# Turning the input in slices 3, 4 and 7 of a chunk instead of 0, 2 and 4

## The chip, the cores and the metric

The kernel runs on one core of one Trainium2 chip. Its time is the device time in microseconds (us). The core has five engines that run side by side, each through its own list of instructions in order: TensorE (PE in the profile; PEld is its loading of weights), VectorE (DVE), ScalarE (ACT), GpSimd (POOL) and SyncE (SP), which here only issues DMAs.

## The reference

The input x is 16 images of 56 x 56 pixels with 384 channels, in float32. Two layers follow each other, each with a residual:

```python
x = x + attention(groupnorm(x), w_qkv, w_proj, b_proj)   # layer 0
x = x + depthwise3x3(groupnorm(x), sign(w))              # layer 1
```

`groupnorm` takes mean and variance of 32 groups of 12 channels over a whole image. The attention projects each pixel to q, k and v (1152 x 384 weights), and lets each pixel look at 3 x 3 neighbours: 12 heads of 32 channels, in three groups with dilations 1, 2 and 3. The softmax runs over the nine neighbours of each head; the weighted sum of v is projected (384 x 384) and added to x. Layer 1 is a 3 x 3 convolution per channel, whose weights are the signs of the given ones.

## The kernel before

**Tiling.** An image is cut into 7 chunks of 8 rows (448 pixels), so there are 112 chunks, `m = 7 b + c` with image b and chunk c. On chip a chunk lies as channels x pixels, in three blocks of 128 channels. Every matmul on 448 pixels in float32 is two PE instructions.

**Stages.** `plan_a` (L402) is stage A: load a chunk of x (pixels on partitions), turn it (`turn`, L420: four PE transposes per channel block into a PSUM tile `pt_x`, a ScalarE copy `xa`, L435, and VectorE's statistics, L436), and write it to DRAM as `xd` (L438). `plan_b` (L446) is stage B: load `xd`, normalise it, project k, v (`pkv`) and q (`pq`, all L464), multiply q by the nine shifted k (L517), sum over channels on PE (the scores, `ps`, L502), softmax (`softmax_1` to `softmax_5`, L529 to L563: the score copy `sT`, PE transposes `pt_s`, L535, maximum, exponential, sum, L544, division, L546, and a split into three bfloat16 terms, on ScalarE and GpSimd), a transposing DMA (`aT`, L568), spreading of the weights to channels on PE (`pb_a`, L581, in nine bursts of three matmuls a chunk), VectorE's product of each burst with v (`w`, L588), GpSimd's adds (L596, L599, L600), the output projection (`po`, L614) and the residual with the statistics of layer 1 (L617, L620). `plan_c` (L648) is stage C: load the result `x1d`, normalise it (L698, L741), convolve (two channel blocks on PE, `pc`, L712; the third on ScalarE and GpSimd, L770 to L786), turn it back (`pt_o`, L793) and store it.

**Order.** Nothing is issued by loop order. `at(when, order, piece)` (L392) puts each piece of work into a table; at the end all pieces are issued by `when`, and within one `when` by `order`, from SOFTMAX (0) to LOADS (14); STAGE_A is 11, behind the projections and ahead of STAGE_C. A chunk has STEP = 9 values of `when`, here called slices 0 to 8. Stage B of chunk m begins at `9 m`, stage C at `9 (m + 10)`, stage A at `start_a(m)`, from the third image on `9 (m - 12)` or one more; so in one round of nine slices PE scores chunk m, turns chunk m + 12 and convolves chunk m - 10. A scheduler then places the issued instructions on each engine's list by its own estimate of times, with the issue order as priority; a list's order is fixed when the program is built.

**Buffers.** The input tile `xin` has one buffer (a second tile is borrowed for the chunks in `doubled`, L852). The three PSUM buffers of `ps_mt` go round among `pt_x`, `pkv`, `po`, `pt_s`, `pc`, `pt_o` and the small tiles of the statistics. `pb_a`, `pq` and `ps` have one PSUM buffer each: a burst of `pb_a` waits until VectorE has multiplied the burst before.

**Statistics.** `statistics` (L858) plans a group norm's finish: aggregating the chunks' statistics (`channels`, L306), then mean, deviation, variance, inversion and spreading, at the distances STAT_SLICE. For the first two images it is planned from the slice of their last turn (L879); for later ones from stage B (L883), together with layer 1's of two images before. It falls into the rounds of c = 0 and c = 1.

Of the kernel before, what the change touches and what calls it, by code (L numbers as in the profile page):

```python
# [20 lines left out]
NG = 3  # L21
# [14 lines left out]
def dilated_attention_then_binary_conv(  # L36
# [31 lines left out]
    NCH = H // ROWS  # L68
# [151 lines left out]
    def turn_qkv_weights(cc):  # L220
        for t3 in range(3):
            pt = ps_mt.tile([P, 512], F32, tag="mt", name="pt_wq")
            for i in range(3):
                nc.tensor.transpose(pt[:, i * P : (i + 1) * P], raw["q", t3][:, i, cc * P : (cc + 1) * P], ident)
            nc.scalar.copy(wqkvT[:, cc, t3 * C : (t3 + 1) * C], pt[:, :C])

    def turn_proj_weights(cc):
        pt = ps_mt.tile([P, 512], F32, tag="mt", name="pt_wp")
        for i in range(3):
            nc.tensor.transpose(pt[:, i * P : (i + 1) * P], raw["p"][:, i, cc * P : (cc + 1) * P], ident)  # L230
        nc.vector.tensor_copy(wprojT[:, cc, :], pt[:, :C])
# [155 lines left out]
    def chunk_of(dram, c):  # L387
        return dram.rearrange("(j p) n -> p j n", p=P)[:, :, c * PX : (c + 1) * PX]
# [3 lines left out]
    def at(when, order, piece):  # L392

        pieces.setdefault((when, order), []).append(piece)
# [7 lines left out]
    def plan_a(m, t0):  # L402

        b, c = divmod(m, NCH)
        had = {}

        def load():
            if c == 0:
                stats0[b] = st_p.tile([P, NG, NCH, 6], F32, tag="stats0", name="stats0")
                xd[b] = dr_p.tile([C, H * W], F32, tag="xd", name="xd")  # L410
            if (b == 0 and c % 3) or m in doubled:

                xin = z_p.tile([P, NQ * PX], F32, tag="z", name="xin_z")[:SUB, : NSUB * C]
                xin = xin.rearrange("p (s c) -> p s c", s=NSUB)
            else:
                xin = xin_p.tile([SUB, NSUB, C], F32, tag="xin", name="xin")
            had["xin"] = xin
            nc.sync.dma_start(xin, xf[b, c * PX : (c + 1) * PX, :].rearrange("(s p) c -> p s c", p=SUB))

        def turn(j):  # L420
            pt = ps_mt.tile([P, 512], F32, tag="mt", name="pt_x")
            for s in range(NSUB):
                nc.tensor.transpose(  # L423
                    pt[:, s * SUB : (s + 1) * SUB], had["xin"][:, s, j * P : (j + 1) * P], ident[:SUB, :SUB]
                )
            if b == 0:

                if j == 0:
                    pool, tag = ((xn_p, "xn"), (xn_p, "xn"), (xn_p, "xn"), (xr_p, "xr"), (t_p, "t"), (w_p, "w"),
                                 (w_p, "w"))[c]  # L430
                    first[c] = pool.tile([P, NG, PX], F32, tag=tag, name="x_first")
                xa = first[c][:, j]
            else:
                xa = xa_p.tile([P, PX], F32, tag="xa", name="xa")
            nc.scalar.copy(xa, pt[:, :PX])  # L435
            nc.vector.bn_stats(stats0[b][:, j, c, :], xa)  # L436
            if b:
                nc.sync.dma_start(xd[b][j * P : (j + 1) * P, c * PX : (c + 1) * PX], xa)  # L438
            elif j == NG - 1:
                nc.scalar.dma_start(chunk_of(xd[b], c), first[c])  # L440

        at(t0 - 3 if b else FIRST + 2 * max(c - 2, 0), LOADS, load)
        for j in range(NG):
            at(t0 + 2 * j if b else FIRST + 2 * c + 1, STAGE_A, lambda j=j: turn(j))

    def plan_b(m, t0):  # L446

# [389 lines left out]
    STAT_ORDER = (STATISTICS, SPREAD, SPREAD, SPREAD, STATISTICS, SPREAD)  # L837
    STEP = 9
    STAT_SLICE = (0, 1, 2, 4, 5, 7)
    FIRST = -200  # L840
    at(FIRST, LOADS, load_weights)
    for cc in range(NG):
        at(FIRST + 6 + 2 * cc, STAGE_C, lambda cc=cc: turn_qkv_weights(cc))
        at(-21 + cc, STAGE_C, lambda cc=cc: turn_proj_weights(cc))
# [9 lines left out]
    def start_a(m):  # L854
        behind = max(m - AHEAD, -2 + m - NCH - len([d for d in doubled if d <= m]))
        return STEP * (behind if m >= NCH else m - 9) + (m in doubled)

    def statistics(when, sets):  # L858

        steps = {}  # L860

        def norm(k, *which):
            if not steps:
                steps["of"] = group_norm([
                    (stats1[b], lambda mr, mrz, b=b: mr1.update({b: (mr, mrz)}), True) if layer
                    else (stats0[b], lambda mr, b=b: mr0.update({b: mr}), False)
                    for layer, b in sets
                ])
            steps["of"][k](*which)

        for n, (layer, _) in enumerate(sets):
            for j in range(NG):

                sooner = 3 - j if n and not layer else 0
                at(when - sooner, STATISTICS, lambda n=n, j=j: norm(0, n, j))
        for k in range(1, 6):
            at(when + STAT_SLICE[k], STAT_ORDER[k], lambda k=k: norm(k))

    for b in range(2):  # L879
        statistics(start_a(NCH * b + NCH - 1) + 5, [(0, b)])  # L880
    for b in range(B):
        last = NCH * b + NCH - 1
        statistics(STEP * last + 27, [(1, b)] + ([(0, b + 2)] if b + 2 < B else []))  # L883
    for m in range(N):
        plan_a(m, start_a(m))
        plan_b(m, STEP * m)
        plan_c(m, STEP * (m + 10))
# [31 lines left out]
```

## Time and profile before

The time is 5223.8 us, the median of three runs (5223.65 to 5231.6). The profiled execution took 5223.35 us.

| | before |
|---|---|
| profiled execution, us | 5223.35 |
| its span, first to last instruction, us | 5221.6 |
| mean granted clock of TensorE | 0.984 |
| busy us of PE, PEld | 5085.7, 2322.5 |
| busy us of DVE, ACT, POOL | 4199.0, 2310.7, 4242.2 |
| turns: PE transposes L423 (1344 in all), us from start to start | 0.095 |
| copies of turns, ACT L435, `xa` x315, mean ns | 534 |
| statistics of turns, DVE L436, median ns | 618 |
| loads of x, L418, 672 KB each, us to landing | 7.3 |

The profile shows one execution. A row of the timeline has the start in us from the span's start, the duration, the engine, the line, the operation with output and inputs, and how many such instructions are merged; a bracket gives the time the engine stood idle before it and what ended that. In the table of waits the columns are total us, times and the longest. PE's instructions overlap, so the distance of two starts tells more than a duration. The forty digits are tenths of busy time in forty equal slices of the span.

### The profile page before, as it was taken

The page shows a single profiled execution, that of the slowest core. Times are in us where ns is not written, and L with a number is a line of the kernel's source. Part 1 is how long each engine was busy: PE and PEld are TensorE (multiplying, and loading weights), DVE is VectorE, ACT ScalarE, POOL GpSimd, SP SyncE. Part 2 cuts the span into 40 slices and gives each one's busy share as a digit, 9 for nine tenths or more (in the row PEclk, how much of TensorE's full clock was granted, in tenths as well). Part 3 has the DMA queues.
Part 4 walks back from the last instruction along what each step waited for, and adds up shares of the span by engine and source line. Part 5 has one row for each costly group of instructions (what it writes and reads, how often), then busy time and mean ns, then how long its engine had stood idle before and what let it go on. Part 6 is the DMA issues. An engine that isn't in the chain of part 4 may idle for free. (4 is left out here: it accounts for less than half of the span.)

```text
span 5221.6 us, 75614 instructions
## 1 busy us (share of the span) xinstructions
PE 5085.7 (97%) x26885; PEld 2322.5 (44%) x26885; DVE 4199.0 (80%) x4125; ACT 2310.7 (44%) x4077; POOL 4242.2 (81%) x2950
## 2 busy tenths in 40 slices
PE   8999999999999999999999999999999999999976
PEld 4444444444444444444444444444444444444433
DVE  4898888888888888888888888888888888878764
ACT  3223444444444544444444444444445444444444
POOL 2677878888888888889888888888888888888881
PEclk8999999999999999999999999999999999999987
DMA  6444656666566565656666565665666656554445
GB/s 197 127 124 119 167 160 166 163 166 167 162 169 165 161 163 159 168 158 166 166 166 165 163 166 162 165 163 160 164 163 171 167 163 168 141 138 135 121 135 158
DMA packets 811631, 825.62 MB, mean 158 GB/s; under 512 B 360307, under 2 KB 801014, under 8 KB 811254
## 3 DMA queue, kind: packets, MB, share of 16 engines
q1 hardware_dynamic: 803270, 808.79, 56.9%
q10 hardware_dynamic: 7984, 12.00, 0.7%
q8 instruction: 213, 3.49, 0.3%
q14 instruction: 164, 1.34, 0.1%
HBM read 466.41 MB, written 231.21 MB: 134 GB/s over the span
## 5 line engine op out<-in xcount | busy, mean ns | idle before, releaser
L596 POOL TENSOR_TENSOR w<-w 128x1344 f32<-128x1344 f32 x672 | 2048.7, 3049 | 327.3 <-DVE w L588 279.1
L517 DVE TENSOR_TENSOR t<-pq,k 128x1344 f32<-128x1344 f32 x1008 | 1528.6, 1550 | 237.8 <-PE pq L464 236.6
L588 DVE TENSOR_TENSOR w<-pb_a,v 128x1344 f32<-128x1344 f32 x1008 | 1560.3, 1548 | 172.6 <-PE pb_a L581 91.9
L464 PE MATMUL pkv<-xn,wqkvT 128*128 128x448 f32 x3924 | 1542.2, 542 | 3.9 <-ACT xa L435 3.5
L464 PEld LDWEIGHTS pkv<-xn,wqkvT 128*128 128x128 f32 x3924 | 725.9, 190 | 664.7 <-issue 634.7
L614 PE MATMUL po<-y,wprojT 128*128 128x448 f32 x2016 | 834.9, 550 | 17.3 <-POOL y L600 17.3
L464 PE MATMUL pq<-xn,wqkvT 128*128 128x448 f32 x1962 | 834.9, 560 | 0.0
L698 ACT ACTIVATE z<-z,mrz 96x448 f32<-96x448 f32 x840 | 573.9, 751 | 266.0 <-DMA z<-x1d 239.7
L777 POOL TENSOR_TENSOR m<-m 128x1344 f32<-128x1344 f32 x210 | 639.1, 3044 | 43.3 <-ACT m L770 37.9
L502 PE MATMUL ps<-t,sel 128*32 128x448 f32 x6048 | 660.8, 546 | 0.3 <-DVE t L517 0.2
L474 ACT COPY v<-pkv 128x448 f32<-128x448 f32 x336 | 178.1, 530 | 918.3 <-PE pkv L464 911.1
L770 ACT ACTIVATE m<-zg,ktap 128x448 f32<-128x448 f32 x945 | 552.6, 658 | 15.1 <-POOL m L777 5.7
L614 PEld LDWEIGHTS po<-y,wprojT 128*128 128x128 f32 x2016 | 376.1, 191 | 374.1 <-issue 347.1
L712 PE MATMUL pc<-z,kdiag 96*32 96x440 f32 (+1 forms) x5040 | 519.3, 545 | 7.1 <-POOL z L700 4.3
L464 PEld LDWEIGHTS pq<-xn,wqkvT 128*128 128x128 f32 x1962 | 345.2, 190 | 318.8 <-issue 318.8
L617 DVE SCALAR_TENSOR_TENSOR xr<-po,bias,xr 128x448 f32<-128x448 f32 x336 | 227.9, 678 | 277.8 <-PE po L614 272.7
L435 ACT COPY xa<-pt_x 128x448 f32<-128x448 f32 x315 | 167.4, 534 | 618.2 <-PE pt_x L423 618.2
L558 POOL TENSOR_TENSOR rest<-ew,e 112x512 f32<-112x512 f32 x112 | 130.1, 1162 | 358.9 <-ACT e L554 358.9
L581 PE MATMUL pb_a<-aT,spread 24*128 24x448 bf16 x3024 | 369.5, 360 | 42.7 <-DVE w L588 36.7
L600 POOL TENSOR_TENSOR y<-y,w 128x448 f32<-128x448 f32 x336 | 381.7, 1136 | 23.8
L599 POOL TENSOR_TENSOR y<-w 128x448 f32<-128x448 f32 x336 | 382.8, 1139 | 19.3
L581 PEld LDWEIGHTS <-spread 24*128 24x128 bf16 x3024 | 100.8, 91 | 621.4 <-issue 603.6
(132 smaller groups left out, 4307.6 us busy)
## 6 DMA issues: line engine op xcount, KB each, us to landing
z<-x1d SPq DMA_DIRECT2D x570, 224.0 KB, 4.0
xr<-xd SPq DMA_DIRECT2D x112, 672.0 KB, 4.3
x1d<-xr SPq DMA_DIRECT2D x112, 672.0 KB, 3.2
xn<-xd SPq DMA_DIRECT2D x109, 672.0 KB, 4.5
xin<-in_x_dram SPq DMA_DIRECT2D x105, 672.0 KB, 7.3
xd<-xa SPq DMA_DIRECT2D x315, 224.0 KB, 3.2
out_dram<-osb SPq DMA_DIRECT2D x420, 168.0 KB, 3.4
x<-x1d SPq DMA_DIRECT2D x112, 448.0 KB, 8.5
```

What stands on the lines that cost most here:

```text
L464: nc.tensor.matmul(dst[:, :PX], wqkvT[:, cc, o0 : o0 + P], had["xn"][:, cc, :], start=(cc == 0), stop=(cc == NG - 1))
L502: return nc.tensor.matmul(had["ps"][32 * j : 32 * j + 32, :PX], sel[:, s0 : s0 + 32], tk, start=(issued[j] == 1), stop=(issued[j] == len(r ...
L517: nc.vector.tensor_tensor(t.rearrange("p k (r w) -> p k r w", w=W), q3, k3, ALU.mult)
L581: return nc.tensor.matmul(pb[:, kx, :PX].rearrange("p (s n) -> p s n", s=NSUB), spread[rows_of, v % 2, :], had["a"][rows_of, :, v // 8, :] ...
L588: nc.vector.tensor_tensor(w.rearrange("p k (r w) -> p k r w", w=W), pb[:, :, :PX].rearrange("p k (r w) -> p k r w", w=W), three(kv[1][g][m ...
L596: nc.gpsimd.tensor_tensor(w0, w0, w, ALU.add)
L599: nc.gpsimd.tensor_tensor(y, w0[:, 0], w0[:, 1], ALU.add)
L614: nc.tensor.matmul(po[:, :PX], wprojT[:, g, j * P : (j + 1) * P], had[f"y{g}"], start=(g == 0), stop=(g == NG - 1))
L698: nc.scalar.activation(z, z, AF.Identity, bias=mrz[:, j, q, 0:1], scale=mrz[:, j, q, 1:2])
L712: return nc.tensor.matmul(pcr[q * HD : (q + 1) * HD, :, lo:hi], kdiag[:, kx, j * NQ + q, :], rows(set_of(j, q))[:, :, lo + kx - 1 : hi + k ...
L770: nc.scalar.activation(rows(t[:, kx]), zp[:, ky : ky + ROWS, kx : kx + W], AF.Copy, scale=ktap[:, o : o + 1])
L777: nc.gpsimd.tensor_tensor(had["m"], had["m"], t, ALU.add)
```

## The change

For all images but the first, the turns of the three channel blocks of a chunk move from slices 0, 2 and 4 after `start_a` to slices 3, 4 and 7, given by the new tuple `TURN_SLICE`. The load of the chunk moves from three slices ahead of `start_a` to `start_a` itself, so that three slices lie between the load and the first turn as before. The group norm of the second image is planned one slice after the last turn, thus at 8 instead of 5; that of the first image stays at 5. What is computed is the same.

```diff
-        at(t0 - 3 if b else FIRST + 2 * max(c - 2, 0), LOADS, load)
+        at(t0 if b else FIRST + 2 * max(c - 2, 0), LOADS, load)
         for j in range(NG):
-            at(t0 + 2 * j if b else FIRST + 2 * c + 1, STAGE_A, lambda j=j: turn(j))
+            at(t0 + TURN_SLICE[j] if b else FIRST + 2 * c + 1, STAGE_A, lambda j=j: turn(j))
...
     STAT_SLICE = (0, 1, 2, 4, 5, 7)
+    TURN_SLICE = (3, 4, 7)
...
     for b in range(2):
-        statistics(start_a(NCH * b + NCH - 1) + 5, [(0, b)])
+        statistics(start_a(NCH * b + NCH - 1) + (TURN_SLICE[NG - 1] + 1 if b else 5), [(0, b)])
```

## The prediction

> **What bounds the kernel now.** I read first the page: busy time by engine, then the forty slices.
>
> ```profile
> PE 5085.7 (97%) x26885; PEld 2322.5 (44%) x26885; DVE 4199.0 (80%) x4125; ACT 2310.7 (44%) x4077; POOL 4242.2 (81%) x2950
> PE   8999999999999999999999999999999999999976
> ```
>
> TensorE (PE) is busy everywhere but at the two ends. A busy PE need not be a PE at its pace, so I turned to the waits of PE alone, between 600 and 4400 us:
>
> ```profile
> PE pb_a L581 <- DVE w L588: 18.4, 14, 1.4
> PE pkv L464 <- ACT xa L435: 3.5, 12, 0.3
> ```
>
> Those 21.9 us are everything PE waited for in 3800 us. Then the timeline of PE: `pt_s` (L535) begins every chunk, so its starts give a chunk's length.
>
> ```profile
> 2748.73 0.60 PE L535 MATMUL pt_s<-perm,sT 128*112 128x128 f32 x4
> ...
> 2792.87 0.49 PE L535 MATMUL pt_s<-perm,sT 128*112 128x128 f32 x3
> ```
>
> 44.14 us. Reading all these starts: in each image from the third on, the rounds in which chunks c = 3, 4, 5, 6 and 0 are softmaxed last 44.14 us to the hundredth (twice slightly more), c = 1 lasts 48.46 (statistics, and one wait of 1.49 us), c = 2 lasts 44.87. A length that repeats so exactly is that of PE's own instruction list. So nothing is gained by making ACT or VectorE lighter as such; each wait put in front of a matmul, and each costlier sequence on PE, is added to the time.
>
> Where does PE come close to waiting? The weigh matmuls (`pb_a`, L581, nine bursts of three a chunk) have one PSUM buffer, so each burst needs the VectorE product `w` (L588) of the burst before. Timeline of a c = 4 round, all engines, around the second burst and around the fifth:
>
> ```profile
> 2754.65 0.61 DVE L546 TENSOR_TENSOR ew<-ew,sm 112x432 f32<-112x432 f32 x1
> ...
> 2755.17 0.62 DVE L436 BATCH_NORM_STATS2 stats<-xa 128x6 f32<-128x448 f32 x1
> 2755.26 1.71 PE L502 MATMUL ps<-t,sel 128*32 128x448 f32 x16
> ...
> 2755.71 1.54 DVE L588 TENSOR_TENSOR w<-pb_a,v 128x1344 f32<-128x1344 f32 x1
> ...
> 2756.78 2.41 PE L712 MATMUL pc<-z,kdiag 96*32 96x448 f32 x24
> ...
> 2759.13 0.36 PE L581 MATMUL pb_a<-aT,spread 24*128 24x448 bf16 x3
> ...
> 2767.46 0.38 PE L793 MATMUL pt_o<-ident,x 128*112 128x128 f32 x2
> 2767.66 0.54 ACT L474 COPY k<-pkv 128x448 f32<-128x448 f32 x1 [1.72 <-PE pkv L464]
> ...
> 2767.88 0.36 PE L581 MATMUL pb_a<-aT,spread 24*128 24x448 bf16 x3
> ...
> 2768.38 1.55 DVE L588 TENSOR_TENSOR w<-pb_a,v 128x1344 f32<-128x1344 f32 x1
> ...
> 2770.35 0.36 PE L581 MATMUL pb_a<-aT,spread 24*128 24x448 bf16 x3
> ```
>
> The first product ends at 2757.25 and burst 2 comes only at 2759.13, behind the convolution `pc`: slack 1.9 us. The fourth product ends at 2769.93, burst 5 starts at 2770.35: slack 0.4 us. Last, VectorE and GpSimd (POOL) in the c = 3 round:
>
> ```profile
> 2710.52 2.18 DVE L546 TENSOR_TENSOR ew<-ew,sm 112x432 f32<-112x432 f32 x1
> ```
> ```profile
> 2709.18 3.05 POOL L596 TENSOR_TENSOR w<-w 128x1344 f32<-128x1344 f32 x1
> ```
>
> The same L546 that took 0.61 us takes 2.18, ending just after POOL's add: it was held. So it is in the c = 3 round of every image from the third to the fourteenth.
>
> [...] a full matmul followed by `pb_a` (24 rows) starts 0.472 us before it instead of 0.376. [...]
>
> **The change, part by part.** I went through the order of the built changed program engine by engine against the old one; the scheduler has moved more than the three turns.
>
> *Work.* Nothing is added or removed: as many transposes, copies, statistics and DMAs.
>
> *PE's list, ordinary round (c = 4, 5, 6, 0; c = 3 alike).* Before: `pt_s, kv, pt_x, pt_o, pb1, pt_o, ps, pc, pb2, pq, pb3, pt_x, pt_o, kv, pt_o, pb4, pt_x, ps, pb5, pc, pb6, pq, kv, po, pb7, po, pb8, ps, pb9, pq, po`. After: `pt_s, kv, pt_o, pb1, pt_o, ps, pb2, pc, pb3, pq, pt_o, kv, pt_x, pt_o, pb4, pt_x, ps, pb5, pc, pb6, pq, kv, po, pb7, po, pt_x, pb8, ps, a third of pq, pb9, the rest, po`. Priced by start-to-start medians of the same sequences (600 to 4400 us): the score run before a burst instead of before `pc` 1.643 against 1.528 (+0.12), `pc` after a burst 2.368 against 2.347 (+0.02); `pq` no longer followed by a burst 2.359 against 2.455 (-0.10); the split `pq` 0.952 + 1.608 against 2.359 (+0.20; c = 2 had this split); turns 0.385 and 0.438 become 0.385 and an estimated 0.48 (+0.04), the `po` ahead of the last 2.359 against 2.455 (-0.10). Sum +0.18: a list of 44.32.
>
> *Burst 2 moves ahead of `pc`.* Times from the start of the round: without the turn (0.385) the scores start at 6.14 and burst 2 could start at 7.78. L546 still ends at 6.53; with the statistics (L436) gone from behind it, `w` 1 follows at once. The old kernel itself shows this at its end, where no turns are left, as in the c = 2 round that starts at 4540.94 (VectorE, then PE):
>
> ```profile
> 4546.86 0.61 DVE L546 TENSOR_TENSOR ew<-ew,sm 112x432 f32<-112x432 f32 x1
> 4547.39 1.55 DVE L588 TENSOR_TENSOR w<-pb_a,v 128x1344 f32<-128x1344 f32 x1
> ```
> ```profile
> 4547.08 1.71 PE L502 MATMUL ps<-t,sel 128*32 128x448 f32 x16
> 4548.99 0.37 PE L581 MATMUL pb_a<-aT,spread 24*128 24x448 bf16 x3 [0.20 <-DVE w L588]
> ```
>
> `w` 1 runs 6.45 to 8.00, burst 2 starts at 8.05. Wait 0.27. The 1.9 us that covered it is gone.
>
> *Turn in slice 3.* Its L436 stands ahead of `w` 4. Now `w` 4 starts 0.92 after the projections end (2767.46 to 2768.38). After: ACT copies `k` at +0.20 to 0.74, `xa` at +0.63 to 1.17; L436 +1.23 to 1.85; `w` 4 +1.77 to 3.32; burst 5 possible at +3.38, while its place in the list is 0.385 + 0.426 + 0.295 + 0.534 + 1.643 = +3.28. Wait 0.10. The other L436 (slice 4) ends at about the time burst 5's product may start; hidden.
>
> *Turn in slice 7.* L436 is ahead of `w` 8: 37.8 to 38.4 on VectorE, `w` 8 to 39.9, burst 9 due at 40.5: hidden, with 0.5 us left, if ACT's `xa` is not late. On ACT it stands behind the four normalisations of `z` (L698), which now start at 34.49 because of their DMA (L685, third issue at 31.26). In the new SP order that issue goes with the two at 24.42 and 24.79, ahead of the `v` halo; ACT is then done by 35, before the turn at 36.9.
>
> *Queues.* SP: the input load (L418) waits for the slice-7 turn, at 37, and the next use is at 18 of the next round, 25 us for a landing of 7.3. The `xd` writes have rounds to spare. POOL puts one add (L596, 3.05) between softmax parts 4 and 5, so the transposing DMA of `aT` issues at some 13.5 instead of 10.4; burst 5 needs it at 21.5: hidden. ACT now normalises `xn` (3 of 0.69) ahead of the score copy `sT`, at worst ending 41.8 against `pt_s` at 44.7: hidden.
>
> Ordinary round: 0.18 + 0.27 + 0.10 = +0.55.
> c = 3: L546 is still held by POOL's add. The row of adds before it starts in the c = 2 round, which grows by some 0.3, and its softmax cast comes 0.3 sooner, so the hold ends near 7.0 instead of 7.66; `w` 1 ends at 8.9, and burst 2 waits about 1.2 where `pc` covered it. +1.5; at the old hold, +2.0.
> c = 2: its old split of `pq` in slice 2 goes; list -0.06, waits +0.37: +0.3.
> c = 1: burst 6 already waits 1.49, because L345 (2.63 us instead of 0.15) is held by the add behind `w` 4. `w` 4 is later by 0.85, PE by 0.385: +0.47, less up to 0.45 of wait at `kv` that ends: +0.2.
> An image: 4 x 0.55 + 1.5 + 0.3 + 0.2 = 4.2; twelve such images, 50.4. The second image, whose c = 3 has no hold, and two last rounds: +4. At the start the matmuls of `pp` pass a turn that waits 3.15 us for its load: -1.4. Sum +53 on the profiled 5223.35 (span 5221.6 plus 1.75 around it, 0.45 under the median of 5223.8): **5277 us**, 1.0% slower.
>
> **Rivals.** *List only*: L546 or the ACT copies come a little sooner than I think, and both small waits vanish. Then +0.18 a round, about +15 to +20: 5240. For it: the waits are 0.27 and 0.10, sums of overlaps of 0.05 to 0.1. Against: VectorE's chain up to L546 isn't touched, and the late rounds wait already.
> *ACT holds the slice-7 turn*: if `z` lands as late as now, in c = 3 `xa` follows at 38.8, `w` 8 ends at 41.5, burst 9 waits 1.3. In c = 4 `z` ends at 37.2, just in time. If it were so in five of seven rounds: 5277 + 12 x 5 x 1.3 = 5355. Against: the earlier issue.
> *Faster*: with L436 out of its way, L345 runs before POOL's add and the c = 1 wait (19.3 us in all) vanishes, the start saves 1.4, and no wait replaces them: 5203. It decides on whether L345 starts within 0.1 us of `w` 4's end. Against: the order of the changed program still has an L436 (slice 4) between them.
> *No change*: the waits of c = 1 to c = 3 fall as much as the list grows: 5224.
>
> **How the numbers follow.** Main case 0.62 (own range 5255 to 5310), list only 0.17, ACT 0.13, faster 0.03, none 0.05. A measurement of this kernel tells about 0.2% (10 us) from no change. List only lies over that bound at 5240, with a fifth of it inside: same 0.08, faster 0.03, slower 0.89. The 80% range takes in list only and part of the ACT case: 5236 to 5335.
>
> **What would show it.** Right: rounds of about 44.7 us instead of 44.14; PE's wait for `w` L588 rising from 18 to some 60 us between 600 and 4400, with its places at burst 2 and burst 5, largest in c = 3; L546 in c = 3 still near 2 us. Wrong: rounds of 44.3 (list only), waits at burst 9 with `xa` behind `z` (ACT), L345 at 0.15 (faster).

## The result, and the profile after

The changed kernel takes 5302.97 us (median of four runs, 5297.28 to 5307.95) against 5226.58 for the kernel before on the same chip (5223.65 to 5231.6). The two medians are 76 us apart, a ratio of 1.0146; the ratio on record is 1.0153, 95% interval 1.0141 to 1.0165. The forecast was +53, 5277, with a range from 5236 to 5335. The profiled execution took 5299.41 us, its span is 5297.7 us, the mean granted clock 0.981.

First the busy times and the slices of PE from the page of the changed kernel:

```profile
PE 5122.6 (97%) x26885; PEld 2337.5 (44%) x26885; DVE 4211.1 (79%) x4125; ACT 2311.8 (44%) x4077; POOL 4234.5 (80%) x2950
PE   8999999999999999999999999999999999999976
```

Nothing is to be seen there: PE is 97% busy again, over a span that is 76 us longer. The waits of PE between 600 and 4400 us say more (total us, times, longest):

```profile
PE pb_a L581 <- DVE w L588: 46.4, 80, 2.5
PE pb_a L581 <- DMA xr<-xd: 3.4, 3, 1.1
```

The first row was 18.4 us in 14 waits. The eighty are one in each round of twelve images but for four c = 3 rounds; those four waits are the second row and one of 1.1 us that the view puts down to another DMA. So PE now waits once in every round, 50.9 us in all, where the forecast had some 60. The timeline of PE gives a round from `pt_s` to `pt_s` (c = 4 of the third image):

```profile
877.52 0.60 PE L535 MATMUL pt_s<-perm,sT 128*112 128x128 f32 x4
...
922.17 0.60 PE L535 MATMUL pt_s<-perm,sT 128*112 128x128 f32 x4
```

44.65 us where it was 44.14. The place of the loss, in the same round, VectorE and PE:

```profile
883.44 0.61 DVE L546 TENSOR_TENSOR ew<-ew,sm 112x432 f32<-112x432 f32 x1
883.97 1.55 DVE L588 TENSOR_TENSOR w<-pb_a,v 128x1344 f32<-128x1344 f32 x1
884.06 1.31 PE L502 MATMUL ps<-t,sel 128*32 128x448 f32 x12
...
885.57 0.37 PE L581 MATMUL pb_a<-aT,spread 24*128 24x448 bf16 x3 [0.20 <-DVE w L588]
...
885.87 2.44 PE L712 MATMUL pc<-z,kdiag 96*32 96x448 f32 x24
```

Burst 2 (885.57) now stands ahead of the convolution `pc`, starts 8.05 us after `pt_s`, and waits for the first product, which runs from 6.45 to 8.00. These are the forecast's three numbers to the hundredth.

All starts of `pt_s` give the whole account of the 76 us. It is made from the spans of the two profiled executions (5221.6 and 5297.7); "undisturbed" is a round without an unusually late hold and without a stretch at half pace, of which more below.

| part | forecast, us | measured, us |
|---|---|---|
| ordinary round (c = 4, 5, 6, 0) | +0.55 | +0.51 |
| c = 1, c = 2, c = 3, undisturbed | +0.2, +0.3, +1.5 | -0.11, +0.32, +1.43 |
| an undisturbed image | +4.2 | +3.65 |
| twelve images, rounds 14 to 97 | +50.4 | +43.8, and +15.0 in disturbed rounds |
| first round's start | -1.4 | -0.5 |
| rounds 0 to 13 (first two images) | within the +4 below | +14.7 |
| rounds 98 to 110 | +4, with the second image | +3.0 |
| sum | +53 | +76.1 (0.1 after the last round) |

So the mechanism was seen, and two terms were missed: the early rounds, and a thing that no row of the forecast had, PE at half its pace.

**The early rounds.** Waits of PE between 90 and 730 us, after:

```profile
PE pb_a L581 <- DMA aT<-e: 8.8, 7, 2.1
```

Before, this row was

```profile
PE pb_a L581 <- DMA aT<-e: 0.8, 1, 0.8
```

The list of GpSimd in round 3 shows where `aT` lost its time. Before:

```profile
223.53 1.16 POOL L558 TENSOR_TENSOR rest<-ew,e 112x512 f32<-112x512 f32 x1 [2.52 <-ACT e L554]
224.75 0.61 POOL L562 CAST e<-rest 112x512 bf16<-112x512 f32 x1
225.44 1.16 POOL L563 TENSOR_TENSOR e<-rest,e 112x512 bf16<-112x512 f32 x1
226.55 3.04 POOL L596 TENSOR_TENSOR w<-w 128x1344 f32<-128x1344 f32 x1
```

After:

```profile
221.20 3.26 POOL L596 TENSOR_TENSOR w<-w 128x1344 f32<-128x1344 f32 x1 [2.64 <-DVE w L588]
224.42 1.15 POOL L558 TENSOR_TENSOR rest<-ew,e 112x512 f32<-112x512 f32 x1
225.54 1.13 POOL L599 TENSOR_TENSOR y<-w 128x448 f32<-128x448 f32 x1
226.62 0.61 POOL L562 CAST e<-rest 112x512 bf16<-112x512 f32 x1
227.19 1.13 POOL L600 TENSOR_TENSOR y<-y,w 128x448 f32<-128x448 f32 x1
228.28 1.16 POOL L563 TENSOR_TENSOR e<-rest,e 112x512 bf16<-112x512 f32 x1
```

The round starts at 216.22 before and at 213.77 after. The last part of the softmax, L563, so ends 10.4 us into the round before and 15.7 after: three adds (L596, L599, L600; 5.5 us together) have moved in front of it. The transposing DMA can only then start, and burst 5 stands waiting. These waits make 8.0 of the 14.7 us. Another 3.4 us come from half pace, which is explained next: PE runs at it for 3.41 us each in rounds 7 and 8, after waits of 2.08 us (for `aT`) and 2.55 us (in a group norm's finish, L339). The kernel before has no half pace in these two rounds.

**Half pace.** Round 24 (c = 3) lasts 49.50 us, while round 17, with the same list, lasts 45.57. Busy time by engine in five adjoining stretches of 3.41 us of round 24 (columns: the stretch, its length, busy us of PE, PEld, DVE, ACT and POOL with the instructions in brackets, PEclk, which is the granted clock, the DMA engines' share and GB/s):

```profile
1153.72:1157.13 3.41, 3.41 (x28) 1.38 (x26) 3.34 (x4) 0.91 (x2) 3.41 (x2) 1.00 0.51 107
1157.13:1160.55 3.42, 1.67 (x19) 0.60 (x19) 2.89 (x3) 1.00 (x2) 2.20 (x5) 1.00 0.72 253
1160.55:1163.96 3.41, 3.41 (x20) 0.80 (x13) 1.37 (x3) 0.00 (x0) 3.41 (x2) 0.50 0.00 0
1163.96:1167.38 3.42, 3.42 (x5) 1.59 (x6) 1.49 (x1) 0.00 (x0) 3.34 (x4) 0.50 0.54 102
1167.38:1170.79 3.41, 3.41 (x12) 1.80 (x11) 2.72 (x2) 0.61 (x2) 2.37 (x1) 1.00 0.93 216
```

In the second stretch PE is busy for 1.67 us only: burst 2 waits. The next two have PE 100% busy at clock 0.50. In the second of them the projections `pq` start 0.75 us apart; in the fifth stretch, at the full clock, those of `pkv` start 0.38 us apart. It ends as sharply as it began. The reason of the long wait itself is in the timeline of the same round, GpSimd, VectorE and PE:

```profile
1154.21 3.06 POOL L596 TENSOR_TENSOR w<-w 128x1344 f32<-128x1344 f32 x1
...
1155.58 2.16 DVE L546 TENSOR_TENSOR ew<-ew,sm 112x432 f32<-112x432 f32 x1
...
1157.66 1.55 DVE L588 TENSOR_TENSOR w<-pb_a,v 128x1344 f32<-128x1344 f32 x1
...
1159.26 0.37 PE L581 MATMUL pb_a<-aT,spread 24*128 24x448 bf16 x3 [1.75 <-DVE w L588]
```

L546 takes 2.16 us, where it took 0.61 in the c = 4 round above: it is held by GpSimd's add, which ends at 1157.27, and itself ends at 1157.74, as foretold for c = 3; but the end of that add isn't fixed. Here it comes 0.64 us later in the round than in round 17 (7.62 against 6.98), after a wait of 0.6 us that GpSimd had for ACT (L770) at the end of the round before. With the convolution as cover such delays cost at most 0.95 us in the kernel before (two c = 3 rounds, of 44.73 and 45.09 us; the others lasted 44.14). Without it, the delay goes straight into PE's list, and can tip PE to half pace.

### The profile page after: what moved, and what is told of

Read it like the earlier page. It is cut to its first block, busy times and chain, and to the rows that moved or that the text cites. A ratio compares the mean times of both kernels' runs of the same rounds, so it can differ in the third digit from the quotient of the medians.

```text
span 5297.7 us, 75700 instructions
## 1 busy us (share of the span) xinstructions
PE 5122.6 (97%) x26885; PEld 2337.5 (44%) x26885; DVE 4211.1 (79%) x4125; ACT 2311.8 (44%) x4077; POOL 4234.5 (80%) x2950
## 5 line engine op out<-in xcount | busy, mean ns | idle before, releaser
L596 POOL TENSOR_TENSOR w<-w 128x1344 f32<-128x1344 f32 x672 | 2050.6, 3052 | 442.1 <-DVE w L588 402.7
L464 PE MATMUL pq<-xn,wqkvT 128*128 128x448 f32 x1962 | 866.2, 569 | 0.0
L770 ACT ACTIVATE m<-zg,ktap 128x448 f32<-128x448 f32 x945 | 552.7, 658 | 18.8 <-POOL m L777 10.2
L798 ACT COPY osb<-pt_o 112x384 f32<-112x384 f32 x420 | 201.9, 481 | 673.1 <-PE pt_o L793 667.2
L600 POOL TENSOR_TENSOR y<-y,w 128x448 f32<-128x448 f32 x336 | 381.7, 1136 | 22.4
L599 POOL TENSOR_TENSOR y<-w 128x448 f32<-128x448 f32 x336 | 382.3, 1138 | 14.1
L581 PEld LDWEIGHTS <-spread 24*128 24x128 bf16 x3024 | 112.0, 91 | 618.9 <-issue 578.4
```

The source lines that it names most:

```text
L464: nc.tensor.matmul(dst[:, :PX], wqkvT[:, cc, o0 : o0 + P], had["xn"][:, cc, :], start=(cc == 0), stop=(cc == NG - 1))
L581: return nc.tensor.matmul(pb[:, kx, :PX].rearrange("p (s n) -> p s n", s=NSUB), spread[rows_of, v % 2, :], had["a"][rows_of, :, v // 8, :] ...
L596: nc.gpsimd.tensor_tensor(w0, w0, w, ALU.add)
L599: nc.gpsimd.tensor_tensor(y, w0[:, 0], w0[:, 1], ALU.add)
L770: nc.scalar.activation(rows(t[:, kx]), zp[:, ky : ky + ROWS, kx : kx + W], AF.Copy, scale=ktap[:, o : o + 1])
```

## The experiments

Each kernel was timed beside the kernel before, whose median was 5222.07 us in the first four comparisons, 5222.75 in the next three and 5221.35 in the last two. The diffs are against the changed kernel. Where the third turn moves, the group norm of the second image moves with it, to one slice later. The table has what their profiles give: rounds in us (median, undisturbed for c = 3), the sum of rounds 0 to 13, and the time at clock 0.50 between 680 and 4450 us.

| turns in slices | time / before | c = 4 | c = 1 | c = 3 | rounds 0-13 | at half pace |
|---|---|---|---|---|---|---|
| 0, 2, 4 (before) | 1 | 44.14 | 48.46 | 44.14 | 582.5 | 3.4 |
| 3, 4, 7 (changed) | 1.0153 | 44.65 | 48.35 | 45.57 | 597.2 | 30.7 |
| 0, 3, 4 | 1.0018 | 44.20 | 48.35 | 44.20 | 586.0 | 13.7 |
| 2, 3, 4 | 1.0164 | 44.45 | 48.91 | 45.6 | 600.5 | 61.4 |
| 3, 4, 7, convolution first | 1.0089 | 44.39 | 50.04 | 44.39 | 597.1 | 37.5 |
| 3, 4, 7, early rounds as before | 1.0123 | 44.65 | 48.34 | 45.6 | 585.3 | 34.1 |
| 0, 4, 7 | 1.0037 | 44.33 | 47.90 | 44.33 | 584.0 | 0 |
| 0, 2, 5 | 1.0005 | 44.36 | 47.07 | 44.36 | 588.6 | 0 |
| 0, 2, 3 | 0.9963 | 44.06 | 47.53 | 44.06 | 581.5 | 0 |
| 3, 5, 7, convolution first | 1.0041 | 44.01 | 46.95 | 44.01 | 600.5 | 0 |

Each profile is of one execution. That of 2, 3, 4 is the slowest of its four (5317.25 us), that of 0, 4, 7 the fastest of its five (5229.08), and those of 0, 2, 3 and of 3, 5, 7 took 5208.31 and 5247.69, some 4 and 5 us above their medians.

**One arrival alone: slice 3.**

```diff
-        at(t0 if b else FIRST + 2 * max(c - 2, 0), LOADS, load)
+        at(t0 - 3 if b else FIRST + 2 * max(c - 2, 0), LOADS, load)
...
-    TURN_SLICE = (3, 4, 7)
+    TURN_SLICE = (0, 3, 4)
```

> Turns in slices 0, 3 and 4, loads as in the kernel before: of the change only the turn in slice 3 is kept, no burst moves past the convolution and no query projection is split. Theory (the change loses at burst 2, in the list and in the early rounds, little at slice 3): ordinary rounds +0.1 us at burst 5, the c = 1 round +0.4 (product 4 is later by 0.85, so burst 6 waits 2.2 instead of 1.5, less the wait at the keys' projection that ends), early rounds as before; 13 x (6 x 0.1 + 0.4) = 13, so 5240, and up to 5255 if PE runs at half its pace after the longer c = 1 waits. GpSimd keeps its old order in the early rounds, so the 14 us that they lost must not appear. Rival (the turn in slice 3, through VectorE, is what delays everything): 5280 or more.

Measured: 5232.36 us, ratio 1.0018 (1.0009 to 1.0027), so +10 rather than +18, and far from the rival's 5280. The ordinary round grows by 0.06, about half of what was expected at burst 5, and c = 1 is 0.11 shorter instead of 0.4 longer. Of the 10 us, half of the 10.2 us more at half pace makes 5. GpSimd's order in the early rounds is the old one, and they lose 3.5 us, not 14. The arrival in slice 3 is not what costs.

**Slice 0 left, no arrival in slice 7.**

```diff
-        at(t0 if b else FIRST + 2 * max(c - 2, 0), LOADS, load)
+        at(t0 - 1 if b else FIRST + 2 * max(c - 2, 0), LOADS, load)
...
-    TURN_SLICE = (3, 4, 7)
+    TURN_SLICE = (2, 3, 4)
```

> Turns in slices 2, 3 and 4, loads one slice before: slice 0 is left, nothing arrives in slice 7. Burst 2 stands ahead of the convolution, the last query projection is not split. Theory (leaving slice 0 is what costs): an ordinary round +0.45 (0.27 at burst 2, 0.1 at burst 5, list +0.08), c = 3 +1.3, the early rounds +14 as in the changed kernel since GpSimd's order is the new one there; 13 x 3.4 + 14 = +58, and 10 more where PE runs at half pace: 5285 to 5297. Rival (the arrival in slice 7, with its split projection and its later copies on ACT, costs most): 5240.

Measured: 5309.31 us, 1.0164 (1.0148 to 1.0180): as slow as the whole change, above both ends of the theory. The rounds are as expected in kind: ordinary +0.31, c = 3 +1.5 undisturbed, rounds 0 to 13 +18. What lifts the sum is half pace: burst 2 of c = 3 starts 1.8 to 3.4 us after the matmul before it, and eight of twelve such rounds last 48.6 to 50.4 us. With 61.4 us at half pace, against 3.4 before, half pace alone costs some 29 us. Leaving slice 0 carries the loss; the rival's 5240 falls.

**The cover given back.**

```diff
-            at(t0 + 14 + i - (pair == 1), WEIGH_AHEAD if pair == 0 else WEIGH, lambda i=i: weigh(i))
+            at(t0 + 14 + i - (pair == 1), WEIGH_AHEAD if pair == 0 and i != 6 else WEIGH, lambda i=i: weigh(i))
```

The burst with i = 6 is burst 2 of the round; issued a class later, it falls behind the convolution again, and all else of the change stays.

> The changed kernel with one burst put back behind the convolution: burst 2 has the convolution's 2.4 us as cover again; turns stay in slices 3, 4 and 7. Theory (the wait at burst 2 without cover, 0.27 us in ordinary rounds and some 1.2 in c = 3): the wait ends, 13 x (4 x 0.3 + 1.2) = 31 us less than the changed kernel: 5272, or 5264 if the half-pace stretches in c = 3 go with it. GpSimd's order in the early rounds is that of the changed kernel, so their 14 us stay. Rival (the list and the later turns cost, not that wait): 5300.

Measured: 5268.04 us, 1.0089 (1.0076 to 1.0103), 33 us less than the changed kernel by the two ratios. The ordinary round falls by 0.26 to 44.39, and c = 3 from 45.57 to the same 44.39: the hold of L546 is hidden again. The waits of PE from 600 to 4400 us fall to

```profile
PE pb_a L581 <- DVE w L588: 24.8, 24, 1.9
```

The early loss stays (597.1 against 597.2), as expected. Unexpected was c = 1: its burst 6 starts 2.39 us after the matmul before it, as in the changed kernel, but here 11 of 12 such rounds last 50.0 us and not 48.35, against 3 of 12. One of them, in stretches of 3.41 us:

```profile
1079.18:1082.59 3.41, 1.55 (x20) 0.44 (x9) 3.38 (x4) 0.00 (x0) 3.12 (x5) 1.00 0.81 256
1082.59:1086.00 3.41, 3.41 (x5) 1.63 (x6) 1.61 (x2) 0.00 (x0) 2.59 (x13) 0.50 0.56 144
1086.00:1089.42 3.42, 3.42 (x10) 1.71 (x9) 2.70 (x2) 0.45 (x1) 3.26 (x3) 1.00 0.00 0
```

PE is busy for 1.55 us of the first and granted half the clock in the second. In the profiles of the kernel before and of the changed kernel the starts of half pace differ by multiples of 3.413 us, to 0.01 us, so they lie on a grid. With the stretch in it, an image of this kernel lasts 317.18 us (median), and 93 steps of the grid are 317.44. So by estimate from these two numbers the wait moves by only some 0.26 us on the grid from one image to the next, and meets the half pace again. An image of the changed kernel that has it in c = 1 alone lasts 319.4, which moves the wait by 2 us. Where the wait lay tells the rounds of the changed kernel apart: each of its twelve c = 1 rounds has a wait of 1.85 to 1.87 us at burst 6. The three with half pace began between 0.07 us before a grid point and 0.08 us after one, so that nearly the whole wait lay in one stretch of the grid; the nine without began from 1.91 to 3.23 us after one.

**The early rounds put back.**

```diff
-        at(t0 if b else FIRST + 2 * max(c - 2, 0), LOADS, load)
+        at(t0 - 3 * (m < OLD) if b else FIRST + 2 * max(c - 2, 0), LOADS, load)
...
-            at(t0 + TURN_SLICE[j] if b else FIRST + 2 * c + 1, STAGE_A, lambda j=j: turn(j))
+            at(t0 + (2 * j if m < OLD else TURN_SLICE[j]) if b else FIRST + 2 * c + 1, STAGE_A, lambda j=j: turn(j))
...
+    OLD = 26
```

The second image's group norm is planned at 5 again.

> The changed kernel, but the chunks that are turned in the rounds 0 to 12 (those numbered below 26 over all images) keep the old slices and the old load time; from round 13 on it is the changed kernel. Theory (the early rounds, without convolution and only some 38 to 42 us long, lose 14 us because GpSimd now adds before it casts the softmax, so that the transposed scores land late): 5303 - 14 = 5289, with the rounds 7 and 8 at 38.6 and 42.0 us again. Rival (the early rounds lose for another reason, a wait for loads that are three slices later or the shift of everything after them): 5300.

Measured: 5284.39 us, 1.0123 (1.0109 to 1.0137), 16 us less than the changed kernel by the two ratios. Rounds 7 and 8 last 38.56 and 42.03 again, and rounds 0 to 13 recover 11.9 of 14.7 us. Of the 2.8 that remain 1.7 are in round 2, 43.52 us against 41.83 in the kernel before (41.41 in the changed kernel), which stays unexplained. So the loss belongs to the early rounds' own lists. That GpSimd's order is behind it, through `aT`, is what the waits above and the runs together point to: the four kernels of the table that leave slice 0 for all images have adds ahead of L562 in the early rounds and lose 14.5 to 18 us there; those that keep it have not, and lie from 1 us below to 6 us above the kernel before. Moving those adds alone wasn't tried, so this cause is argued and not isolated.

**The other arrival alone: slice 7.**

```diff
-        at(t0 if b else FIRST + 2 * max(c - 2, 0), LOADS, load)
+        at(t0 - 2 if b else FIRST + 2 * max(c - 2, 0), LOADS, load)
...
-    TURN_SLICE = (3, 4, 7)
+    TURN_SLICE = (0, 4, 7)
```

> Turns in slices 0, 4 and 7, loads two slices before: of the change only the arrival in slice 7 is kept. Burst 2 stays behind the convolution, the last query projection is split around burst 9. Theory (slice 7 costs only its place in PE's list): the split +0.20, the turns +0.04, the output projection -0.10, so +0.14 in an ordinary round and about as much in c = 2 and c = 3, nothing in c = 1, whose last query projection isn't split; 13 x 0.85 = +11: 5233, no wait at burst 9, early rounds as before. Rival (the copies of the turn on ACT, behind the normalisations, or the later statistics hold product 8 or 9): 5260 or more.

Measured: 5245.5 us, 1.0037 (1.0024 to 1.0049). The ordinary round is +0.19 where +0.14 was expected, c = 1 is 0.56 shorter, where no change was expected. In the c = 6 rounds something of the rival shows: they last up to 45.56 instead of 44.33, with a wait of up to 1.16 us at burst 9, the copy of the turn on ACT (L435) behind a normalisation of `xn` (L460) that waited for its load. It is 3.8 us over twelve images, not the tens it would take. The times of the five runs lie between 5229 and 5248, and the profile is that of the fastest. Hence a second one.

> The kernel with turns in slices 0, 4 and 7 once more, for a second profile: its five times lie between 5229 and 5248, and the one that was profiled was the fastest. Theory (waits behind the turn in slice 7, with ACT's normalisations and their loads ahead of it, differ from one execution to the next): if the time is near 5245, rounds with c = 6 above 44.8, or more of them, and waits at burst 9. Rival (stretches at half pace that fall otherwise on the grid): half-pace stretches in the c = 1 rounds or elsewhere. A time near 5229 again tells neither.

Measured: 5243.85 us, a span 14.7 us above that of the first profile. The c = 6 rounds give 0.8 of it. The last thirteen rounds give 11.3: in the c = 3 rounds 101 and 108 burst 2 starts 2.9 us after the matmul before it in both profiles, and in these thirteen rounds PE ran at half pace for 34.1 us instead of 10.2. The list and the waits at burst 2 are the same; that the waits lay at another place on the grid is my estimate. So it is the rival's half pace, not in the c = 1 rounds but in its "elsewhere".

**The third turn out of slice 4.**

```diff
-    TURN_SLICE = (3, 4, 7)
+    TURN_SLICE = (0, 2, 5)
```

The load is at `t0 - 3` again, here and in the next kernel.

> Turns in slices 0, 2 and 5, loads as in the kernel before. With no turn in slice 4 the scheduler puts the scores and the convolution ahead of burst 5, and no statistics of a turn stand between product 4 and L345. Theory (the 1.5 us of the c = 1 round come from L345, held by the GpSimd add behind product 4, with burst 6 waiting for product 5 queued behind it): burst 5 and 6 now have the convolution as cover, so the wait ends even if L345 is still held; 13 x 1.5 = 19, another 3 for the stretches at half pace, and 0.04 a round in the list: 5196 to 5200. Rival (the hold only moves on to a later burst): 5222 or above.

Measured: 5224.32 us, 1.0005 (0.9997 to 1.0013): no gain, though the c = 1 round is 1.4 us shorter, as expected. Its VectorE, GpSimd and PE:

```profile
1692.93 1.56 DVE L588 TENSOR_TENSOR w<-pb_a,v 128x1344 f32<-128x1344 f32 x1 [0.93 <-POOL dev L333]
...
1694.37 2.49 PE L712 MATMUL pc<-z,kdiag 96*32 96x448 f32 x24
1694.40 0.14 DVE L342 TENSOR_SCALAR var<-pv 32x2 f32<-32x2 f32 x1
1694.56 3.04 POOL L596 TENSOR_TENSOR w<-w 128x1344 f32<-128x1344 f32 x1 [2.53 <-DVE var L342]
1694.57 3.05 DVE L345 TENSOR_SCALAR var<-var 32x2 int32<-32x2 int32 x1
1696.80 0.36 PE L581 MATMUL pb_a<-aT,spread 24*128 24x448 bf16 x3
...
1699.86 0.37 PE L581 MATMUL pb_a<-aT,spread 24*128 24x448 bf16 x3 [0.24 <-DVE w L588]
```

The product in the first row is the fourth. L345 stands directly behind L342 and starts 0.08 us after the fourth product's end; GpSimd's add starts 0.01 us sooner, and L345 is held for all of it. PE's wait at burst 6 (1699.86) is down to 0.24 us all the same, because PE has the convolution to do before burst 5 (1696.80). In twelve images that is 16.7 us. What took the gain back is another wait of PE, in the ordinary rounds:

```profile
PE ps L502 <- DVE t L517: 16.5, 61, 0.3
```

With the turn gone from ahead of the scores, PE reaches them up to 0.3 us before VectorE's products `t` are there, 61 times. The early rounds lose another 6.1 us, which was not followed up.

**The same with slice 3.**

```diff
-    TURN_SLICE = (3, 4, 7)
+    TURN_SLICE = (0, 2, 3)
```

> Turns in slices 0, 2 and 3: as the run with 0, 2 and 5, but the third turn stands ahead of burst 4. Theory: the same end of the c = 1 wait, 5196 to 5203; product 4 is later by some 0.85 us behind two statistics, but burst 5 has the scores and the convolution as cover, so the 0.1 us of slice 3 is hidden. Rival (the statistics ahead of product 4 delay the row of products after it and with it the adds on GpSimd, whose hold of L546 in c = 3 lasts longer): 5215 to 5230.

Measured: 5204.6 us, 0.9963 (0.9949 to 0.9976): faster than both kernels, by 0.4% of the kernel before, and just above the expected 5196 to 5203. PE no longer waits for `t`, as the turn in slice 3 now stands ahead of the scores; the ordinary round is 44.06, c = 1 47.53, there is no half pace from 680 to 4450 us, and PE's waits for `w` from 600 to 4400 us are

```profile
PE pb_a L581 <- DVE w L588: 8.2, 12, 0.7
```

Some of the gain is lost again at the end: rounds 98 to 110 take 582.2 us against 576.8 before, with more half pace (41.5 us against 23.9 between 4450 and 5050 us).

**Half pace taken away.**

```diff
-            at(t0 + 14 + i - (pair == 1), WEIGH_AHEAD if pair == 0 else WEIGH, lambda i=i: weigh(i))
+            at(t0 + 14 + i - (pair == 1), WEIGH_AHEAD if pair == 0 and i != 6 else WEIGH, lambda i=i: weigh(i))
...
-    TURN_SLICE = (3, 4, 7)
+    TURN_SLICE = (3, 5, 7)
```

> The run in which burst 2 stands behind the convolution again, with the second turn moved on from slice 4 to slice 5. In that run the c = 1 round lasted 50.04 us in eleven images of twelve: burst 6 started 2.39 us after the matmul before it, and PE then ran at half its pace for 3.41 us. Theory (half pace follows where some 1.8 us of PE's idle time fall into one window of a grid of 3.41 us; without the long interval it can't): with the turn out of slice 4 the scores and the convolution stand ahead of burst 5, the interval ends, c = 1 lasts some 47.2 and no image has a half-pace stretch there: 5268 - 12 x 2.8 = 5234. Rival (half pace comes with the length of the list or the load on the chip, not with the wait): a stretch of half pace stays in most images, 5250 or more.

Measured: 5242.31 us, 1.0041 (1.0027 to 1.0054). No stretch at half pace is left between 680 and 4450 us, and c = 1 lasts 46.95: the theory of the wait holds. The sum misses by 8 us. The turn in slice 7 now meets a new wait, of the output projection for a PSUM buffer that ACT's copy has to free, mostly in c = 6 (44.2 to 46.0 us in the twelve images):

```profile
PE po L614 <- ACT xa L435: 6.9, 10, 1.9
```

Beside it there are now small waits for `w` in the rounds of c = 0 and c = 4 to 6 (7.0 us), mostly at burst 9.

## Why the prediction was partly right

**The list and the two waits** of the ordinary round held, and the experiments give each alone. Burst 2 without its cover costs 44.65 - 44.39 = 0.26 (forecast 0.27 and 0.04 of list). The arrival in slice 7 costs 0.19 (forecast 0.14), that in slice 3 0.06 (forecast 0.10). They add up to the 0.51 measured. The step that named the lost 1.9 us of `pc` as the main thing is shown by the run that gives it back.

**c = 3** was right for an undisturbed round, +1.43 for +1.5. Its step "the hold ends near 7.0" is true of round 17 (6.98), but the hold's end varies by 1.4 us from image to image (8.40 in round 73), and each such delay is now paid by PE.

**c = 1** had the wrong sign, by 0.3 a round. The wait at burst 6 grew as forecast, from 1.95 to 2.40 us from start to start. But product 4 is not later: PE has one turn less before burst 4 and the wait for the keys has ended, so product 4 starts 20.53 us into the round instead of 21.01, and the longer wait only uses up what PE had gained.

**The early rounds** are the first failed step: "the transposing DMA of `aT` issues at some 13.5 instead of 10.4; burst 5 needs it at 21.5: hidden". This was worked out for a round of 44 us, with one add in front of L563, and it is right there. Rounds 3 to 7 have no convolution and lasted 38.6 us; there three adds come first, L563 ends at 15.7, and burst 5 is due at 19.7 or sooner. "The second image and two last rounds: +4" hence became +14.7 for rounds 0 to 13 and +3.0 for the last thirteen.

**The missing term** is half pace. Disturbed rounds cost +15.0 over the twelve images; the clock itself makes (30.7 - 3.4) / 2 = 13.7 of it, the rest is the longer waits of a late hold. Its sign is in the profile of before, and the prediction passed over it: round 57 (c = 1) lasted 50.15 instead of 48.46 there. The forecast priced a wait at its own length; in the changed kernel, between 680 and 4850 us, a wait that left PE busy for 1.77 us or less of such a stretch of 3.41 us cost, in all cases but one, another 1.7 us (48.35 to 50.05) or, with two stretches at half pace, about 3.4 us (half of 6.83).

That the sum missed by only 23 us is in part luck: the twelve images without the disturbed rounds were forecast 6.6 us too dear, and no part of the range stood for the early rounds or for half pace.

**Rivals.** *List only* falls: both small waits are there. *ACT holds the slice-7 turn* falls for the changed kernel: ACT's waits for `z` fell from 199.0 to 73.7 us between 600 and 4400 us, as the step on the earlier issue said, and no burst 9 of the twelve images waits; the run with turns in 0, 4 and 7 shows a weak form of it through `xn`. *Faster* falls twice: the statistics still stood ahead of L345, and even without them, with L345 0.08 us behind product 4, inside the 0.1 us that I named as the deciding point, GpSimd was first. The gain came in the end another way, by cover for burst 5. In the round shown for turns in 0, 2 and 5, L345 takes 3.05 us and ends at 1697.62, 0.02 us after the add. In the kernel before all fourteen L345 of 32x2 elements end 0.02 us after the add beside them and take 2.63 to 3.07 us; the four of 32x1 take 0.13 to 0.14, one of them (4826.06) with an add beside it that had started 0.01 us sooner. Why the one form is held and the other not, no run here shows.

## What to carry to other kernels

Read what stands between a matmul and the product it needs: moving a cheap thing (here a turn of 0.4 us) can let the scheduler swap two big ones, and it was the cover of 2.4 us that was lost, not the 0.4. Check a "hidden" on every kind of round, the short ones at the start too, not only on the one that fills most of the time. Prefer an order in which PE's waits are many and small over one with a wait near 2 us; the fastest of the orders tried has no wait over 0.7 us between 600 and 4400 us. That alone is not enough: the order 0, 2, 5 has no wait over 0.3 us there, and is no faster than the kernel before.

## What the hardware showed that was not expected

PE drops to half its clock inside a stream that is 97% busy: in the changed kernel for 30.7 us between 680 and 4450 us. All starts of half pace in its profile lie on multiples of 3.413 us from one another, to 0.01 us, and so do those in the profile of the kernel before. PE need not be idle for a whole stretch of this grid: the wait of 1.75 us in the row of round 24 above, which lay in one stretch, was followed by half pace. Between 680 and 4850 us of the changed kernel seven stretches at full clock were followed by it. In all of them PE was busy for 1.77 us or less. One other stretch with so little (1.73 us, from 3635.21) was not followed by it, and no stretch with 1.81 us or more was. So the border is about half the stretch in this profile, and the same wait of 1.87 us cost 1.7 us or nothing by where it fell. (The ends of matmuls are modelled in the profile, so these busy times are not exact.) Of the seven, half pace lasted one stretch in three and two in four; what decides between these was not found.

The kernel before shows that the border is not sharp. Five of its c = 1 rounds have a stretch of the grid in which PE is busy for 2.00 us. Four of these stretches were not followed by half pace; the one in round 57, with a wait of 1.41 us in it, was:

```profile
2634.29:2637.70 3.41, 2.00 (x20) 0.74 (x13) 3.37 (x5) 0.00 (x0) 3.12 (x5) 1.00 0.79 228
2637.70:2641.12 3.42, 3.42 (x6) 1.65 (x5) 1.33 (x1) 0.00 (x0) 2.60 (x14) 0.50 1.09 225
```

And a stretch of the same profile with 1.95 us busy (from 4593.54) was not followed by it. So PE's busy time in one stretch does not decide alone.
